# Layer 1 of a two-layer graph network: the end of a group in pairs of row tiles, 22 sums by transfer, head 3's last sum on GpSimd, and earlier loads of the row factors

## The chip, the core and the metric

The kernel runs on one core of one Trainium2 chip. A core has five engines with instruction streams of their own: TensorE (PE in the profile; PEld is its weight load), VectorE (DVE), ScalarE (ACT), GpSimd (POOL) and SyncE (SP), and 16 DMA engines that they share. A compute engine does its instructions in the order of its own stream. So does a queue of DMA issues: a DMA that has to wait for a semaphore holds back what stands behind it on the engine that issues it. The metric is device time in microseconds (us), from start to end of one execution.

## The reference

Layer 0 takes `x` (4096 x 512) and `adj` (4096 x 4096, zeros and ones) through a graph layer; the change doesn't touch it. Layer 1 is graph attention with 8 heads of 64 channels:

```python
h = relu(layernorm(x))
data1 = (h @ W.T + b).reshape(N, H, D)          # N = 4096, H = 8, D = 64
src = einsum('nhd,xhd->nh', data1, src_proj)
trg = einsum('nhd,xhd->nh', data1, trg_proj)
e = src.T[:, :, None] + trg.T[:, None, :]       # one number per head, row and column
e = where(e >= 0, e, 0.01 * e) + adj            # adj is added to the logits
scores = softmax(e, axis=-1)
out = einsum('hnm,hmd->hnd', scores, data1.transpose(1, 0, 2))
x = x + out                                     # heads side by side
```

## The kernel before

Layer 1 never forms the scores of all heads at once. It goes through 8 *groups*: 4 blocks of 1024 output rows (`WL`), each with 2 sets of 4 heads (`HG`). A group has 32 *steps* (`NT`), one for each tile of 128 columns `m`. In a step the kernel makes four unnormalised weight tiles `pr[i, m, k]`, 128 columns by 1024 rows, one for each head `k` of the set, and TensorE multiplies them with the values and adds up over the 32 steps in PSUM. The leaky relu under an exponential is a maximum of two products, so that a weight is `max(z, g) * exp(e)`, up to a factor of the column: `z` is a *row factor* (1024 numbers repeated on all partitions, one tile for each head, read again in all 32 steps), and `g` is one number per partition.

What each engine does in a step:

- SP (`load`, line 700): fetches the tile `e` of the adjacency for three steps ahead, into one of three buffers. A few steps also load the row factors of the next group (`zload`, line 695) or the row `u` (line 705). There are two sets of `z` tiles, used by groups in turn.
- ACT: `ex = exp(e)` (`exps`, line 718) into a single buffer in PSUM, so it can start only when VectorE has finished the step before; then, one step further ahead, `e3` (line 728), the same with head 3's factor of the column in it, and `rl` (line 746), a relu for head 0. In the first two groups it also scales two heads of the values (line 714).
- DVE (`weigh`): the four weight tiles in the order 3, 0, 1, 2 (lines 757 and 760). The instruction for head 3 reads `z` and `e3` from SBUF; the three others read `ex` from PSUM.
- In four steps, `BY_LOG`, head 0's tile is made without VectorE: ACT makes a relu of `u` (line 735), a DMA on GpSimd's queue adds the adjacency to it (line 736, issued five steps ahead), and ACT takes the exponential into `pr0` (line 743). VectorE then has three instructions in that step.
- POOL: adds head 3's tile to a running sum `acc3` (lines 767 and 769). For most steps it also issues a DMA that adds head 0's tile to one of two running sums in SBUF, by turns (`BY_DMA`, lines 774 and 776). `pr0` has three buffers, the other heads' tiles have two.
- PE (`gather`): 16 matmuls of 32 output columns for the product (line 792, "pv"), head pairs (3, 0) first, then (1, 2), and 4 with two output columns for the denominators of heads 1 and 2 (line 797, "dn"). Each is recorded as two. Four of them, in four column groups of the array, run side by side. For the steps that aren't in `BY_DMA` head 0's denominator is added here too, by two more matmuls for two of the four column groups (`by_pe`); which two alternates (`side`), and the order of the product's matmuls follows it. In the last step come head 3's last tile and the three running sums.

The program's order is written out by hand. A step `s` issues, in this order, `load` 3 steps ahead, `logs` 5, `exps` 1, `weigh` 1, `factors` 2, `scale` 2 and `gather` 0, and then the next piece of the end of the group before:

```python
stages = ((load, 3), (logs, 5), (exps, 1), (weigh, 1), (factors, 2), (scale, 2), (gather, 0))
```

The end of a group is spread over the first steps of the next one. At the end of `gather` ACT copies the product out of PSUM (line 821). `denominators` then copies the sums, turns them by eight small matmuls (line 831) and takes reciprocals on VectorE (line 835). After that `finish` works on 8 row tiles: `turn` (line 847) transposes one with two matmuls into the PSUM tile `pt`, which has one buffer, ACT multiplies its four heads by the reciprocals in the next step (line 871), GpSimd's queue adds the residual `x1` to two row tiles by one DMA (line 874), and SP stores them three steps later (line 877). In `finish` one row tile goes through in each of steps 2 to 9. The last group has its own end, `finish_last`, where PE turns all row tiles at once and ACT and VectorE share the scaling; tiles 4 to 7 lie in two PSUM banks.

Of the kernel before, what the change touches and what calls it, by code (L numbers as in the profile page):

```python
# [28 lines left out]
def kernel(  # L29
# [602 lines left out]

    HV = WL // BL
    JT = BL // P
    Q = P // 4
    BY_LOG = (17, 21, 25, 29)
    BY_DMA = [m for m in range(2, NT - 5) if m % 4 != 1]  # L640

    with tc.tile_pool(name="p", bufs=2) as prp, tc.tile_pool(name="rl", bufs=2) as rlp, tc.tile_pool(
        name="io1", bufs=3
# [48 lines left out]
        def zload(i, k):  # L692
            b, g = groups[i]
            zs_[i, k] = (zp1 if i % 2 else zp0).tile([P, WL], FP, name=f"z{k}")
            nc.sync.dma_start(zs_[i, k], row_bcast(z_d, WL, (g * HG + k) * N + b * WL))

        def load(i, m):
            b, g = groups[i]
            e = ep.tile([P, WL], FP, name="e")
            nc.sync.dma_start(e, adj_t[m * P:(m + 1) * P, b * WL:(b + 1) * WL])  # L700
            ra[i, m] = e
            if i + 1 < len(groups) and m == 28:
                us[i + 1] = usp.tile([P, WL], FP, name="u")
                b, g = groups[i + 1]
                nc.sync.dma_start(us[i + 1], row_bcast(u_d, WL, g * N + b * WL))
            if i + 1 < len(groups) and m in (20, 22, 24, 26):
                zload(i + 1, ORDER[(m - 20) // 2])

        def scale(i, m):

# [38 lines left out]
        def weigh(i, m, order=ORDER):  # L749
# [15 lines left out]
            if m == 1:  # L765
                acc[i, 3] = acp.tile([P, WL], FP, name="acc3", bufs=1)
                nc.gpsimd.tensor_tensor(acc[i, 3], pr[i, 0, 3], w, ALU.add)
            elif 1 < m < NT - 1:
                nc.gpsimd.tensor_tensor(acc[i, 3], acc[i, 3], w, ALU.add)  # L769
            if m in BY_DMA:  # L770
                n = BY_DMA.index(m)
# [6 lines left out]
        def gather(i, m):  # L778
# [26 lines left out]
                for q in range(HV):  # L805
                    den(side * HV + q, zo[:, 1 - side:3], pr[i, m, 0], q, start=False, stop=False)
            if last:
                for q in range(HV):
                    den(HV + q, zo[:, 1:3], pr[i, m, 3], q, start=False, stop=False)
                for q in range(HV):  # L810
                    den(q, zo[:, 1:3], acc[i, 0, 1], q, start=False, stop=False)
                for r, a in enumerate((acc[i, 0, 0], acc[i, 3])):
                    for q in range(HV):
                        den(r * HV + q, zo[:, 1:3], a, q, start=False, stop=True)
# [41 lines left out]
        def finish(i):  # L856


            dens = denominators(i)
            os_ = next(dens)  # L860
            yield
            next(dens)
            yield
            rd = next(dens)
            pts, os2 = {}, {}
            for t in range(WT + 4):
                if 0 < t <= WT:
                    if t % 2:
                        o = iop.tile([P, 2, HG, D], FP, name="o")
                    for r, k in enumerate(ORDER):  # L870
                        nc.scalar.activation(o[:, (t - 1) % 2, k, :], pts[t - 1][:, r, :], AF.Copy,
                                             scale=share(rd, t - 1, r))
                    if t % 2 == 0:
                        nc.gpsimd.dma_start(o, part(x1, i, t - 2, 2), accum_op=ALU.add)
                        os2[t] = o
                if t - 3 in os2:
                    nc.sync.dma_start(part(out, i, t - 5, 2), os2[t - 3])
                if t < WT:
                    pts[t] = p_t.tile([P, HG, D], FP, name="pt")
                    turn(os_, t, pts[t])  # L880
                yield

        def finish_last(i):

# [5 lines left out]
            os_ = next(dens)  # L890
            pts = [p_v.tile([P, HG, D], FP, name=f"pv{c}{q}") for q in range(HV) for c in range(2)]
            xs = p_x.tile([P, 4, HG, D], FP, name="ex")
            pts += [xs[:, n, :, :] for n in range(4)]
            for t in range(4):
                turn(os_, t, pts[t])
            next(dens)
# [115 lines left out]
```

## Time and profile before

The median of three runs is 2970.18 us (2969.84 to 2971.4). The profiled execution took 2974.0 us; its span, from the first instruction to the last, is 2972.2 us.

| | before |
|---|---|
| median of the runs | 2970.18 us |
| the profiled execution, its span | 2974.0 us, 2972.2 us |
| VectorE's first weight tile of layer 1 starts at | 1742.05 us |
| groups 0 to 7 start at (VectorE, head 3, step 0) | 1742.05, 1894.46, 2046.95, 2196.78, 2349.36, 2499.29, 2651.82, 2801.81 us |
| last step of the last group starts at | 2947.60 us |
| busy over the span: PE, DVE, ACT, POOL | 99%, 85%, 45%, 46% |
| DMA share of the time in groups 1 to 6 | 0.83 to 0.84 |

A start is that of VectorE's instruction for head 3, with which each step begins. The shares over the whole span mix two layers with different limits, so layer 1 is read by itself: busy times of the engines over whole groups, and the times of the steps within a group. PE's busy time counts a matmul from its modelled start to its modelled end, and neighbours overlap; how long a step takes PE is read from the start of one step's first matmul to that of the next. Records of a DMA issue stand on the engine that issues it; the landing is told separately.

### The profile page before, as it was taken

How to read it: one execution, taken by the hardware profiler on the slowest of the kernel's cores; microseconds unless marked ns; L12 is line 12 of the kernel's file. 1: busy time of each engine (PE TensorE's matmuls, PEld its weight loads, DVE VectorE, ACT ScalarE, POOL GpSimd, SP SyncE). 2: the span in 40 equal slices, each digit the busy share in tenths (PEclk: the TensorE clock that was granted, in tenths of full speed). 3: DMA queues.
4: the chain of work that ended last, by engine and by line, in shares of the span. 5: the costliest groups of instructions: out<-in, count | busy, mean ns of one | idle time of the engine just before them, and what ended most of it. 6: DMA issues, size and time to landing. Idle time of an engine off the chain costs nothing.

```text
span 2972.2 us, 43109 instructions
## 1 busy us (share of the span) xinstructions
PE 2930.7 (99%) x15371; PEld 1159.4 (39%) x15371; DVE 2522.1 (85%) x3596; ACT 1326.1 (45%) x1852; POOL 1376.0 (46%) x1042
## 2 busy tenths in 40 slices
PE   8999999999999999999999989999999999999998
PEld 4444444444444444444444423323222322232222
DVE  5434777778888888888897789999999999999998
ACT  2121111111122122122122368888777777777776
POOL 3401111113444444444443656575757575757574
PEclk9999999999999999999999999999999999999999
DMA  4205666667976675665553149696969696979795
GB/s 155 96 7 179 223 222 219 230 219 184 208 180 172 159 177 173 157 175 177 155 179 99 54 138 239 183 255 192 251 196 247 201 248 202 241 206 240 209 230 154
DMA packets 454056, 552.02 MB, mean 186 GB/s; under 512 B 261624, under 2 KB 287256, under 8 KB 453840
## 3 DMA queue, kind: packets, MB, share of 16 engines
q1 hardware_dynamic: 400816, 387.81, 42.2%
q0 software_dynamic: 51008, 157.51, 23.0%
q10 hardware_dynamic: 2016, 3.93, 0.4%
q8 instruction: 121, 1.98, 0.3%
q14 instruction: 95, 0.78, 0.1%
HBM read 409.47 MB, written 59.97 MB: 158 GB/s over the span
## 4 chain that ended last, share of the span: by engine, by line
PE 85%; DVE 6%; DMA 4%; ACT 2%; issue 2%; POOL 1%; SPq 0%; DVEq 0%; ACTq 0%; POOLq 0%
PE po L437 30%; PE pv L792 20%; PE pe L288 15%; PE dn L797 7%; DVE pr L760 5%; PE ps L159 4%; PE po L507 4%; PE pe L166 4%; DMA acc<-pr 2%; DMA e<-in_adj_t_dram 1%; DVE pr L757 1%; PE pt L847 1%; ACT e L728 1%; POOL acc L769 1%; ACT ex L718 0%
## 5 line engine op out<-in xcount | busy, mean ns | idle before, releaser
L792 PE MATMUL pv<-pr,sup 128*32 128x512 f32 x8192 | 1010.4, 595 | 10.3 <-POOL d_m L957 5.4
L437 PE MATMUL po<-sup,at 128*128 128x512 f32 x2048 | 886.7, 594 | 2.2 <-DVE at L407 2.2
L769 POOL TENSOR_TENSOR acc<-acc,pr 128x1024 f32<-128x1024 f32 x232 | 559.2, 2410 | 315.4 <-DVE pr L760 314.9
L760 DVE SCALAR_TENSOR_TENSOR pr<-z,g_m,ex 128x1024 f32<-128x1024 f32 x512 | 630.7, 1272 | 7.9 <-ACT ex L718 7.5
L437 PEld LDWEIGHTS po<-sup,at 128*128 128x128 f32 x2048 | 387.4, 190 | 480.7 <-issue 446.1
L417 POOL TENSOR_TENSOR racc<-racc,ex 128x512 f32<-128x512 f32 x240 | 358.3, 1493 | 390.7 <-ACT ex L401 389.0
L792 PEld LDWEIGHTS pv<-pr,sup 128*32 128x32 f32 x8192 | 288.5, 110 | 594.6 <-issue 528.2
L401 ACT ACTIVATE ex<-d 128x512 f32<-128x512 f32 x256 | 160.5, 630 | 664.7 <-DVE d L399 648.1
L288 PE MATMUL pe<-he_t,he_t 128*128 128x512 f32 x896 | 386.4, 592 | 0.0
L718 ACT ACTIVATE ex<-e 128x1024 f32<-128x1024 f32 x256 | 263.0, 1027 | 219.7 <-DVE pr L760 219.4
L760 DVE SCALAR_TENSOR_TENSOR pr<-z,g_m,e 128x1024 f32<-128x1024 f32 x256 | 328.3, 1282 | 9.3 <-PE pv L792 5.4
L797 PE MATMUL dn<-pr,d_m 128*2 128x512 f32 x1984 | 335.4, 592 | 0.0
L728 ACT ACTIVATE e<-e,ld_m 128x1024 f32<-128x1024 f32 x256 | 291.3, 1138 | 17.7 <-DMA e<-in_adj_t_dram 17.5
L757 DVE SCALAR_TENSOR_TENSOR pr<-rl,ngd_m,ex 128x1024 f32<-128x1024 f32 x224 | 284.8, 1271 | 1.9 <-ACT ex L718 1.5
L746 ACT ACTIVATE rl<-z,ngd_m,d_m 128x1024 f32<-128x1024 f32 x224 | 275.1, 1228 | 0.0
L407 DVE TENSOR_TENSOR at<-ex,a 128x512 f32<-128x512 f32 x256 | 195.3, 763 | 80.0 <-ACT ex L401 51.2
L288 PEld LDWEIGHTS pe<-he_t,he_t 128*128 128x128 f32 x896 | 169.2, 190 | 210.1 <-issue 190.5
L291 ACT COPY es<-pe 128x512 f32<-128x512 f32 (+2 forms) x144 | 79.3, 551 | 377.0 <-PE pe L288 377.0
L292 POOL DMA_DIRECT2D e_d<-es x144 | 78.5, 545 | 364.7 <-ACT es L291 359.2
L399 DVE TENSOR_TENSOR d<-pt,mk 128x512 f32<-128x512 f32 x256 | 176.9, 691 | 8.8
L293 DVE CUSTOM_DVE_ANT_0 mk<-pe,mk 128x512 f32<-128x512 f32 (+2 forms) x144 | 93.0, 646 | 99.3 <-ACT es L291 99.3
L392 DVE TENSOR_SCALAR mk<-a 128x512 f32<-128x512 f32 x256 | 136.5, 533 | 1.9 <-DMA a<-in_adj_t_dram 1.9
(173 smaller groups left out, 2595.0 us busy)
## 6 DMA issues: line engine op xcount, KB each, us to landing
e<-in_adj_t_dram SPq DMA_DIRECT2D x256, 512.0 KB, 5.5
acc<-pr POOLq DMA_DIRECT2D x152, 512.0 KB, 5.8
a<-in_adj_t_dram SPq DMA_DIRECT2D x256, 256.0 KB, 3.3
ar<-in_adj_dram SPq DMA_DIRECT2D x120, 256.0 KB, 3.1
e_d<-es POOLq DMA_DIRECT2D x120, 256.0 KB, 3.1
eb<-e_d SPq DMA_DIRECT2D x456, 64.0 KB, 2.7
ac<-in_adj_t_dram SPq DMA_DIRECT2D x112, 256.0 KB, 3.6
et<-e_d SPq DMA_DIRECT2D x112, 256.0 KB, 3.4
```

Of the source, the lines that this page charges most:

```text
L288: nc.tensor.matmul(pe[:, :w], he_t[i][:, k, (t % TB) * P:(t % TB + 1) * P], he_t[j][:, k, BL - w:], start=(k == 0), stop=(k == KC - 1))
L407: nc.vector.tensor_tensor(w, e, aj.pop((b, m)), ALU.mult)
L417: nc.gpsimd.tensor_tensor(racc, racc, e, ALU.add)
L437: nc.tensor.matmul(po[j], w[:, j * P:(j + 1) * P], sup[:, m, :], start=(m == 0), stop=last)
L718: nc.scalar.activation(x_, ra.pop((i, m)), AF.Exp)
L728: nc.scalar.activation(x_, ra[i, m], AF.Exp, bias=ld_m[:, h // HG, m:m + 1])
L746: nc.scalar.activation(r, zs_[i, 0], AF.Relu, bias=ngd_m[:, h // HG, m:m + 1], scale=d_m[:, h, m:m + 1])
L757: nc.vector.scalar_tensor_tensor(w, rl.pop((i, m)), ngd_m[:, h // HG, m:m + 1], x_, op0=ALU.subtract, op1=ALU.mult)
L760: nc.vector.scalar_tensor_tensor(w, zs_[i, k], g_m[:, h + k, m:m + 1], e3.pop((i, m)) if k == 3 else x_, op0=ALU.max, op1=ALU.mult)
L769: nc.gpsimd.tensor_tensor(acc[i, 3], acc[i, 3], w, ALU.add)
L792: nc.tensor.matmul(v[c][q][r * D + c0:r * D + c0 + Q, :], va[:, m, g * HG + k, c0:c0 + Q], pr[i, m, k][:, q * BL:(q + 1) * BL], start=(m = ...
L797: nc.tensor.matmul(dn[r * Q:r * Q + w.shape[1], :], w, src[:, q * BL:(q + 1) * BL], **fl)
```

## The change

Five things are changed, all in layer 1:

1. `BY_DMA` goes from 19 of the 32 steps to 22: all of 2 to 29 but 9, 13, 15, 18, 22 and 26. The steps whose denominator of head 0 is left to PE are now 0, 1, 9, 13, 15, 18, 22, 26, 30 and 31 (before: 0, 1, 5, 9, 13, 17, 21, 25 and 27 to 31).
2. `BY_LOG` moves from steps 17, 21, 25, 29 to 16, 20, 24, 28.
3. The row factors of the next group are loaded along with the tiles `e` of steps 1 to 4 (steps 21 to 24 in group 0), and not with 20, 22, 24 and 26.
4. GpSimd adds head 3's tile of step 31 to `acc3`; the two matmuls that PE had for it are gone.
5. `finish` takes row tiles by pairs, every third step: four transposes after steps 2, 5, 8 and 11, into a `pt` of twice the size; the scaling of one tile in each of the two steps that follow; the residual's DMA in steps 4, 7, 10 and 13; the stores in steps 6, 9, 12 and 15. In `finish_last` the row tiles 4 to 7 are placed so that 4 and 6 share one bank of PSUM and 5 and 7 the other.

```diff
-    BY_LOG = (17, 21, 25, 29)
-    BY_DMA = [m for m in range(2, NT - 5) if m % 4 != 1]
+    BY_LOG = (16, 20, 24, 28)
+    BY_DMA = [m for m in range(2, NT - 2) if m not in (9, 13, 15, 18, 22, 26)]
...
-            if i + 1 < len(groups) and m in (20, 22, 24, 26):
-                zload(i + 1, ORDER[(m - 20) // 2])
+            m0 = 1 if i else 21
+            if i + 1 < len(groups) and m0 <= m < m0 + 4:
+                zload(i + 1, ORDER[m - m0])
...
-            elif 1 < m < NT - 1:
+            elif m > 1:
                 nc.gpsimd.tensor_tensor(acc[i, 3], acc[i, 3], w, ALU.add)
...
             if last:
                 for q in range(HV):
-                    den(HV + q, zo[:, 1:3], pr[i, m, 3], q, start=False, stop=False)
-                for q in range(HV):
                     den(q, zo[:, 1:3], acc[i, 0, 1], q, start=False, stop=False)
...
-            pts, os2 = {}, {}
-            for t in range(WT + 4):
-                if 0 < t <= WT:
-                    if t % 2:
-                        o = iop.tile([P, 2, HG, D], FP, name="o")
-                    for r, k in enumerate(ORDER):
-                        nc.scalar.activation(o[:, (t - 1) % 2, k, :], pts[t - 1][:, r, :], AF.Copy,
-                                             scale=share(rd, t - 1, r))
-                    if t % 2 == 0:
-                        nc.gpsimd.dma_start(o, part(x1, i, t - 2, 2), accum_op=ALU.add)
-                        os2[t] = o
-                if t - 3 in os2:
-                    nc.sync.dma_start(part(out, i, t - 5, 2), os2[t - 3])
-                if t < WT:
-                    pts[t] = p_t.tile([P, HG, D], FP, name="pt")
-                    turn(os_, t, pts[t])
+            old = None
+            for t in range(0, WT, 2):
+                pt = p_t.tile([P, 2, HG, D], FP, name="pt")
+                for j in range(2):
+                    turn(os_, t + j, pt[:, j, :, :])
+                yield
+                o = iop.tile([P, 2, HG, D], FP, name="o")
+                for j in range(2):
+                    for r, k in enumerate(ORDER):
+                        nc.scalar.activation(o[:, j, k, :], pt[:, j, r, :], AF.Copy, scale=share(rd, t + j, r))
+                    if j == 0:
+                        if t:
+                            nc.sync.dma_start(part(out, i, t - 2, 2), old)
+                        yield
+                nc.gpsimd.dma_start(o, part(x1, i, t, 2), accum_op=ALU.add)
+                old = o
                 yield
+            yield
+            nc.sync.dma_start(part(out, i, WT - 2, 2), old)
+            yield
...
-            pts += [xs[:, n, :, :] for n in range(4)]
+            pts += [xs[:, n, :, :] for n in (0, 2, 1, 3)]
```

## The prediction

> **What bounds the kernel now.** The page first: over the whole span PE looks like the bound.
>
> ```profile
> span 2972.2 us, 43109 instructions
> ...
> PE 2930.7 (99%) x15371; PEld 1159.4 (39%) x15371; DVE 2522.1 (85%) x3596; ACT 1326.1 (45%) x1852; POOL 1376.0 (46%) x1042
> ```
>
> That average mixes the layers. The second view is the busy time in windows that are one group of layer 1 each (group 1, and the sum of 1 to 6; columns: us, PE, PEld, DVE, ACT, POOL, clock, DMA share, GB/s).
>
> ```profile
> 1894.46:2046.95 152.49, 151.93 (x1380) 47.85 (x1376) 149.10 (x127) 130.49 (x199) 95.23 (x57) 1.00 0.84 221
> ...
> sum 907.35, PE 906.44 PEld 273.19 DVE 893.68 ACT 714.48 POOL 570.97; mean PE 151.07 PEld 45.53 DVE 148.95 ACT 119.08 POOL 95.16
> ```
>
> Two engines are full: a group takes 907.35 / 6 = 151.2 us, PE is busy for 151.1, VectorE for 149.0. The timelines tell which leads where. On VectorE:
>
> ```profile
> 2252.09 1.27 DVE L757 SCALAR_TENSOR_TENSOR pr<-rl,ngd_m,ex 128x1024 f32<-128x1024 f32 x1
> 2253.30 2.47 DVE L760 SCALAR_TENSOR_TENSOR pr<-z,g_m,ex 128x1024 f32<-128x1024 f32 x2
> 2256.43 1.28 DVE L760 SCALAR_TENSOR_TENSOR pr<-z,g_m,e 128x1024 f32<-128x1024 f32 x1 [0.66 <-PE pv L792]
> ```
>
> Undisturbed, weight tiles start 1.193 us apart, a step takes 4.77 and a step by logs (three tiles) 3.58. The floor of a group is 28 x 4.77 + 4 x 3.58 = 147.9 us, and the last line shows one of the gaps above it, a wait for PE. Subtracting the floor from the start of each step on this timeline gives an excess of 4.5, 4.6, 1.9, 4.7, 2.0, 4.6, 2.1 and 2.6 us in groups 0 to 7, 26.9 together. It lies in four places (sums over groups): step 0 and 1 4.9 and 1.5, steps 7 to 12 7.6, steps 21 to 29 9.3, the reciprocal in step 3 1.3; the rest is 0.05 to 0.1 after each step by logs. The change removes no VectorE work, so it can win these gaps and the tail, no more.
>
> PE's timeline shows why step 11 has a gap (the starts of "pv" x32 are the starts of steps 9 and 10 of group 4; step 8 started at 2395.31):
>
> ```profile
> 2400.11 3.64 PE L792 MATMUL pv<-pr,sup 128*32 128x512 f32 x32
> 2403.57 1.04 PE L797 MATMUL dn<-pr,d_m 128*2 128x512 f32 x8
> 2404.43 1.03 PE L797 MATMUL dn<-pr,zo 128*3 128x512 f32 x4
> 2405.39 0.44 PE L847 MATMUL pt<-ident,os 128*128 128x128 f32 x2
> 2405.75 3.64 PE L792 MATMUL pv<-pr,sup 128*32 128x512 f32 x32
> ```
>
> A step with two transposes takes 4.80 us, with a denominator of head 0 as well 5.64; steps 11 and 12 without either take 4.29. So a pair of transposes costs 0.51 (the transposes start 0.11 apart at the tail, eight in 1.09; the rest is emptying the array) and a denominator 0.85. Where no transposes lie between two denominators on opposite column groups, they share one 0.85: step 13 takes 4.30 and step 17 5.14. PE falls behind VectorE from 4.9 us (step 1) to 8.1 (step 10); at about 7.5 head 3's buffers run out.
>
> Waits in layer 1, and DMA issues in a quiet stretch (2332 to 2358 us) and in the stretch with the row factors (2430 to 2480; last number: us to landing):
>
> ```profile
> ACT e L728 <- DMA e<-in_adj_t_dram: 17.5, 22, 1.9
> ...
> DVE pr L760 <- ACT ex L718: 7.5, 9, 1.9
> ...
> ACT pr L743 <- DMA acc<-pr: 7.1, 8, 2.0
> ```
>
> ```profile
> e<-in_adj_t_dram SPq DMA_DIRECT2D x6, 512.0 KB, 3.9
> ```
>
> ```profile
> e<-in_adj_t_dram SPq DMA_DIRECT2D x11, 512.0 KB, 8.3
> acc<-pr POOLq DMA_DIRECT2D x8, 512.0 KB, 8.8
> z<-z_d SPq DMA_DIRECT2D x4, 512.0 KB, 9.9
> ```
>
> The gaps of steps 21 to 29 come from here: with row factors under way everything lands twice as late, ACT waits for `e` or for `pr0` to be read out, and VectorE for ACT. Group 7, which loads none, has no gap in steps 13 to 29 beyond 0.06 after each step by logs.
>
> **The change, part by part.**
>
> *PE.* Before, the denominators cost ten times 0.85 a group: 0 with 1, 5, 9, four pairs (13/17, 21/25, 27/28, 29/30), and three rounds in step 31. After, seven: 0 with 1, 9 (step 11's transposes part it from 13), 13/15, 18/22, 26/30, two rounds in step 31 (31's own is on the other column groups). That is 3 x 0.85 = 2.6 us less. Transposes: 8 x 0.51 = 4.1 become 4 x (0.51 + 2 x 0.11) = 2.9. PE's group goes from 151.1 to 151.1 - 2.6 - 1.2 = 147.3, under VectorE's floor, so PE stops setting the pace: steps 7 to 12 lose their gap (7.6, all of it in groups 1 to 7). The cover is the lag: it rises by 0.9 to step 3 and falls 3.2 below the start by step 28, then rises; from the least lag seen, 2.8 in group 0, the peak is near 6, short of 7.5.
>
> *Head 3's last sum on GpSimd.* Step 1's head 3 tile waits now until PE has read head 3's tile of step 31 for the denominators (gap 0.4 to 0.8). Afterwards that buffer is free after the product. GpSimd is idle for 12.4 us at this place, its sum takes 2.4 and ends 3.7 after step 31 starts; PE needs it some 8 after. ACT's four copies out of PSUM (2.0 us) stay: ACT's step of 3.13 + 2.02 = 5.15 is longer than 4.77, and 0.27 of the gap stays. Saved: 0.2 to 0.5 in each of groups 1 to 7.
>
> *Loads of the row factors.* They leave the crowded steps and go behind the `e` loads at the seam of two groups, where an `e` lands in 3.9 us and has 9.4 (from its issue to head 3's exponential). On SP's queue the first waits for VectorE's head 3 tile of step 31, 0.1 later than the `e` behind it could start: nothing. The seven loads of `u` stay. Three more sums by DMA come, 0.6 of a step's DMA time each; four row factors of about 0.2 go from the crowd. I count the gaps of steps 21 to 29 in groups 1 to 6 as gone (7.2) but 0.7 in group 1, where ACT also scales values. In group 0 the loads come in four steps running, in the crowd: unchanged, 4.5.
>
> *The end by pairs.* VectorE's reciprocal stays, 0.18. ACT: an undisturbed step costs 3.13, four scalings 0.90, a relu for the logs 1.04. The relu for step 16 is issued in step 11, right behind the scalings of step 10: 5.07 + 0.11 against 4.77. Step 12 gets a new gap of about 0.26; group 1 has 0.55 of value scaling on top there and at the seam, 1.2 in all. Stores: SP now meets each one two steps after the residual's DMA, not three. That DMA took 4.1 or 8.0 us, the longer behind a sum; all four are behind a sum now. SP is held to 7.7 us into the next step, the `e` queued there could start at 6.0, so it goes 2.1 late and must land in 7.3. It landed in 5 to 8 in those steps: 0.3 a group.
>
> *The tail.* PE ends nearer VectorE: the lag of 5.33 us in the last step becomes some 3.6, and one round of 0.85 is gone: 2.5. The order of PSUM tiles 4 to 7 saves nothing: ACT's and VectorE's waits on one another stand in the changed program as before; 1.5 at best if they fell.
>
> **Weighing a rule.** Row: in step 17 of group 3 GpSimd's sum began late, behind a DMA issue, and ran on after VectorE's head 3 tile had started; that one took 1.94 instead of 1.28 and ended 1.10 after the sum.
>
> ```profile
> 2283.97 1.94 DVE L760 SCALAR_TENSOR_TENSOR pr<-z,g_m,e 128x1024 f32<-128x1024 f32 x1
> ```
>
> The Trainium skill, page "SBUF — State Buffer", section "Who interferes with whom", says why: a VectorE instruction with two inputs in SBUF and a GpSimd instruction that reads SBUF exclude each other for a whole instruction. By that rule the added sum speaks against the change, up to 2.4 us in each of 8 groups, 19 us, if it fell on a head 3 tile; by the row's times it ends 1.1 us before the next one starts, so it costs nothing, and the 0.06 after each step by logs stays.
>
> **Sum.** Groups 2 to 6: floor 147.88 + 0.18 + 0.27 + 0.26 + 0.25 (four steps after logs) + 0.3 = 149.1, five times; group 1: 151.0; group 0: 152.4; group 7 to the start of its last step: 149.1 - 4.77 = 144.3. Together 1193.2 against 2947.60 - 1742.05 = 1205.6: 12.4 less, with the tail 14.9. The profiled execution goes from 2974.0 to about 2959.1; the median stands 3.8 below it, so 2955.3. Bounds: every gap gone but group 0's start and the reciprocals, tail 3.5: 27 less, 2943. Gaps of steps 21 to 29 all kept: 6.5 worse, 2962.
>
> **Rivals.**
>
> 1. *The transfers stay late.* 22 sums instead of 19 put back what the row factors took out. For: steps 14 to 16 already show a DMA share near 0.95 with a sum and an `e` in each. Against: there the sums landed in 5 to 6 us, and they have 7.9 before ACT's `pr0`. 2962.
> 2. *Slower: SP stuck behind the stores.* If the residual's DMA lands at its worst seen, 9.9 us, the `e` behind goes 4 late and at 8 us to landing comes 2.6 after ACT wants it; ACT can absorb 1.5 of its idle time a step. 28 stores at 1.1 are 31 us against the 15 won: 2986. It decides against the change from 0.55 us a store on. For: stores already waited 20.0 us for the residual in 16 of 28 cases. Against: the longest such wait was 2.7, and the crowd thins.
> 3. *Nothing changes.* PE's relief is real but each freed gap is taken by ACT, whose step is 4.0 to 5.2 us in the first twelve steps: 2968 to 2972.
> 4. *All gaps go*: 2946.
>
> **How the numbers follow.** Main case 0.62, first rival 0.15, second 0.10, third 0.08, fourth 0.05. Within 0.2% (5.9 us) is what a measurement of this kernel can't tell from no change: 2964.2 to 2976.1. Faster 0.80 (main, fourth, most of the first), same 0.10, slower 0.10. The range leaves out the second rival, most of the third and the far end of the fourth: 2945 to 2966. The likeliest time is 2955.
>
> **What would show it.** Groups 2 to 6 of about 149 us with VectorE busy to 99% and PE showing waits for it; no wait of VectorE for PE in steps 8 and 12; `e` under 7 us to landing in steps 17 to 27; about 0.2 us before VectorE's second tile in steps 1 and 12; a tail of 22 us after the last step's start, not 24.6. Wrong if VectorE still waits for PE (my lag is off), if ACT waits for `e` behind the stores, or if a head 3 tile takes 1.9 us in each group.

## The result, and the profile after

The changed kernel takes 2978.70 us (median of 9 runs, 2975.83 to 2982.48) against 2970.66 (9 runs, 2969.73 to 2971.92): a ratio of 1.0028, 95% interval 1.0018 to 1.0038. It is slower by 8 us; 2955 was forecast, 15 faster. The profiled execution took 2979.28 us.

First the page of the changed kernel.

```profile
span 2977.5 us, 42931 instructions
...
PE 2918.4 (98%) x15243; PEld 1149.5 (39%) x15243; DVE 2521.6 (85%) x3596; ACT 1323.3 (44%) x1852; POOL 1411.3 (47%) x1074
```

PE lost 12 us of busy time and the span grew by 5. Where it grew shows in the windows of groups 2 and 3 and the sum of groups 1 to 6 (us, PE, PEld, DVE, ACT, POOL, clock, DMA share, GB/s).

```profile
2049.87:2202.43 152.56, 150.22 (x1356) 43.82 (x1356) 148.91 (x127) 116.37 (x137) 100.22 (x61) 1.00 0.91 233
2202.43:2353.64 151.21, 149.26 (x1356) 43.37 (x1356) 148.92 (x127) 116.28 (x137) 100.34 (x61) 1.00 0.91 233
...
sum 914.36, PE 899.55 PEld 264.08 DVE 893.69 ACT 711.98 POOL 601.25; mean PE 149.92 PEld 44.01 DVE 148.95 ACT 118.66 POOL 100.21
```

VectorE's work is what it was (893.69 against 893.68), but the six groups take 914.36 instead of 907.35. The DMA share rose from 0.83 or 0.84 to 0.90 or 0.91. So VectorE waits more, and no longer for PE. The waits of the changed kernel in layer 1 (us in total, times, longest):

```profile
PEld pv L792 <- DVE pr L760: 85.8, 147, 1.2
...
ACT e L728 <- DMA e<-in_adj_t_dram: 33.2, 26, 4.0
ACT pr L743 <- DMA acc<-pr: 24.6, 13, 3.0
DVE pr L760 <- ACT ex L718: 20.6, 20, 2.1
```

The kernel before had in the same list:

```profile
PEld pv L792 <- DVE pr L760: 27.3, 85, 1.1
...
DVE pr L760 <- PE pv L792: 5.4, 10, 0.7
```

VectorE's wait for PE (5.4 us before) is gone from the list, and PE's weight loads wait for VectorE for 85.8 us (27.3 before). In its place ACT waits for transfers: for the tile `e` 33.2 us against 17.5, for the sums of head 0 24.6 against 7.1, and VectorE waits for ACT (20.6 us against 7.5). The chain that ended last says the same. By line, its shares of the span, in the kernel before and in the changed one:

```profile
PE po L437 30%; PE pv L792 20%; PE pe L288 15%; PE dn L797 7%; DVE pr L760 5%; PE ps L159 4%; PE po L507 4%; PE pe L166 4%; DMA acc<-pr 2%; DMA e<-in_adj_t_dram 1%; DVE pr L757 1%; PE pt L847 1%; ACT e L728 1%; POOL acc L769 1%; ACT ex L718 0%
```

```profile
PE po L437 30%; PE pe L288 15%; DVE pr L760 10%; PE pv L792 6%; DMA acc<-pr 4%; PE ps L159 4%; PE po L507 4%; PE pe L166 4%; DMA e<-in_adj_t_dram 3%; ACT e L728 3%; PE dn L797 2%; DMA o<-x 2%; POOL acc L769 1%; ACT ex L718 1%; DVE pr L757 1%
```

The product of layer 1 (`pv`) had 20% and has 6; the sums by transfer went from 2 to 4%, `e` from 1 to 3, and the residual's transfer is new there.

By steps, the excess over VectorE's floor (the time of the steps beyond their undisturbed lengths, as in the prediction) is 37.0 us in the eight groups, where it was 26.9. Two places hold what is new. **Steps 20 and 28** have 13.9 (nothing before): these are logs steps now. **Steps 10 to 16** have 9.9, of which 1.9 in step 12 are ACT's as forecast; these are the steps of the stores. The gaps of steps 7 and 11 for PE are gone.

The first place, in group 2, on the timeline (start, us, engine and line, tiles; releaser in brackets):

```profile
2165.38 0.86 POOL L736 DMA_DIRECT2D lg<-in_adj_t_dram  x1 [0.27 <-ACT lg L735]
...
2169.03 0.86 POOL L776 DMA_DIRECT2D acc<-pr  x1
...
2172.68 0.85 POOL L776 DMA_DIRECT2D acc<-pr  x1
...
2183.63 1.15 ACT L743 ACTIVATE pr<-lg,t_m 128x1024 f32<-128x1024 f32 x1 [2.98 <-DMA acc<-pr]
...
2185.72 2.47 DVE L760 SCALAR_TENSOR_TENSOR pr<-z,g_m,ex 128x1024 f32<-128x1024 f32 x2 [1.24 <-ACT ex L718]
```

```profile
2172.68 10.77 DMA acc<-pr
```

Step 24, a logs step, is short (3.58 us). GpSimd's queue issues the logs' transfer for step 28, the sum of step 24 and the sum of step 25 within 7.3 us. The last of them lands after 10.77 us (second fence, from the chain). Head 0's tiles have three buffers, so step 28's goes over step 25's, which that sum reads, and ACT wanted it 2.98 us earlier; its `ex`, on which VectorE waits 1.24 us, stands behind.

The second place, also in group 2: SP's queue.

```profile
2102.32 0.39 SPq L875 DMA_DIRECT2D out_dram<-o  x1
...
2102.81 6.46 SPq L699 DMA_DIRECT2D e<-in_adj_t_dram  x3
...
2107.26 1.44 POOL L877 DMA_DIRECT2D o<-x  x1
...
2111.46 1.15 ACT L728 ACTIVATE e<-e,ld_m 128x1024 f32<-128x1024 f32 x1 [2.55 <-DMA e<-in_adj_t_dram]
...
2117.78 0.39 SPq L875 DMA_DIRECT2D out_dram<-o  x1
...
2118.28 6.26 SPq L699 DMA_DIRECT2D e<-in_adj_t_dram  x3
```

The store of 2117.78 follows a residual issued at 2107.26 that landed 10.51 us later, and two `e` loads come in a bunch behind it; behind the store before it, an `e` was 2.55 us late for ACT. Over all groups, what the stores waited for (the second line is a group's last store):

```profile
SPq L875 <- DMA o<-x: 155.7, 21, 8.4
SPq L881 <- DMA o<-x: 50.4, 7, 7.8
```

That is 206 us in all 28 cases; before it was 20.0 in 16. The `e` load behind a store was issued 3.2 us after its buffer had come free, on average over the 28; in the kernel before 0.03.

### The profile page after: what moved, and what is told of

It reads as the page before. It is cut to its first block, busy times and chain, and to the rows that moved or that the text cites. A ratio compares the mean times of both kernels' runs of the same rounds, so it can differ in the third digit from the quotient of the medians.

```text
span 2977.5 us, 42931 instructions
## 1 busy us (share of the span) xinstructions
PE 2918.4 (98%) x15243; PEld 1149.5 (39%) x15243; DVE 2521.6 (85%) x3596; ACT 1323.3 (44%) x1852; POOL 1411.3 (47%) x1074
## 4 chain that ended last, share of the span: by engine, by line
PE 65%; DVE 12%; DMA 10%; ACT 7%; issue 4%; POOL 2%; SPq 0%; DVEq 0%; ACTq 0%; POOLq 0%
PE po L437 30%; PE pe L288 15%; DVE pr L760 10%; PE pv L792 6%; DMA acc<-pr 4%; PE ps L159 4%; PE po L507 4%; PE pe L166 4%; DMA e<-in_adj_t_dram 3%; ACT e L728 3%; PE dn L797 2%; DMA o<-x 2%; POOL acc L769 1%; ACT ex L718 1%; DVE pr L757 1%
## 5 line engine op out<-in xcount | busy, mean ns | idle before, releaser
L792 PE MATMUL pv<-pr,sup 128*32 128x512 f32 x8192 | 1025.7, 595 | 21.7 <-DVE pr L760 10.3
L769 POOL TENSOR_TENSOR acc<-acc,pr 128x1024 f32<-128x1024 f32 x240 | 584.4, 2435 | 318.4 <-DVE pr L760 316.6
L760 DVE SCALAR_TENSOR_TENSOR pr<-z,g_m,ex 128x1024 f32<-128x1024 f32 x512 | 630.8, 1272 | 20.9 <-ACT ex L718 20.6
L797 PE MATMUL dn<-pr,d_m 128*2 128x512 f32 x1984 | 343.9, 592 | 0.0
L728 ACT ACTIVATE e<-e,ld_m 128x1024 f32<-128x1024 f32 x256 | 291.2, 1137 | 33.4 <-DMA e<-in_adj_t_dram 33.2
L776 POOL DMA_DIRECT2D acc<-pr x160 | 148.9, 931 | 0.1
```

The lines of the kernel that those rows point to most:

```text
L728: nc.scalar.activation(x_, ra[i, m], AF.Exp, bias=ld_m[:, h // HG, m:m + 1])
L760: nc.vector.scalar_tensor_tensor(w, zs_[i, k], g_m[:, h + k, m:m + 1], e3.pop((i, m)) if k == 3 else x_, op0=ALU.max, op1=ALU.mult)
L792: nc.tensor.matmul(v[c][q][r * D + c0:r * D + c0 + Q, :], va[:, m, g * HG + k, c0:c0 + Q], pr[i, m, k][:, q * BL:(q + 1) * BL], start=(m = ...
L797: nc.tensor.matmul(dn[r * Q:r * Q + w.shape[1], :], w, src[:, q * BL:(q + 1) * BL], **fl)
```

## The experiments

All times are medians. "Beside" is the kernel before on the same chip; the chip differs between the groups of runs, so differences are taken to that. An "excess" is that of the profiled execution, by steps as in the prediction. Theory A is the first place (sums of the logs steps late), theory B the second (stores on SP's queue), theory C the whole transfer load.

| kernel | us | beside | ratio (95%) | excess |
|---|---|---|---|---|
| changed | 2978.70 | 2970.66 | 1.0018 to 1.0038 | 37.0 |
| changed, sums as before | 2967.34 | 2971.86 | 0.9971 to 0.9989 | 20.0 |
| changed, end as before | 2969.21 | 2971.86 | 0.9985 to 1.0002 | 23.8 |
| changed, logs steps by PE | 2963.38 | 2971.86 | 0.9956 to 0.9980 | 21.1 |
| changed, stores later | 2972.07 | 2971.86 | 0.9992 to 1.0010 | 29.2 |
| both of these | 2960.63 | 2971.13 | 0.9952 to 0.9979 | 16.9 |
| both, group 0's loads spread | 2959.58 | 2971.13 | 0.9949 to 0.9974 | 16.2 |
| changed, loads as before | 2988.67 | 2971.13 | 1.0047 to 1.0073 | 49.3 |
| before, loads alone | 2972.36 | 2971.13 | 0.9993 to 1.0011 | 25.9 |
| changed, steps after logs by PE | 2971.86 | 2971.94 | 0.9993 to 1.0010 | 27.2 |
| before, head 3's sum alone | 2970.70 | 2971.94 | 0.9989 to 1.0007 | 23.8 |
| before, 22 sums alone | 2980.03 | 2971.94 | 1.0019 to 1.0042 | 36.6 |
| before, pairs alone | 2970.18 | 2971.94 | 0.9989 to 1.0007 | 21.2 |
| steps after logs by PE, stores later | 2959.61 | 2971.67 | 0.9946 to 0.9973 | 17.8 |
| before, 22 sums, logs steps by PE | 2963.51 | 2971.67 | 0.9963 to 0.9986 | 18.3 |
| both, loads spread, end as before | 2959.14 | 2971.67 | 0.9945 to 0.9970 | 16.0 |

### Which part loses

The 19 sums and the logs steps of before, in the changed kernel:

```diff
-    BY_LOG = (16, 20, 24, 28)
-    BY_DMA = [m for m in range(2, NT - 2) if m not in (9, 13, 15, 18, 22, 26)]
+    BY_LOG = (17, 21, 25, 29)
+    BY_DMA = [m for m in range(2, NT - 5) if m % 4 != 1]
```

> The changed kernel with parts 1 and 2 undone: BY_DMA and BY_LOG as before, 19 sums by transfer. Theory A (the sums of the logs steps go by transfer now: the logs DMA, the sum of the logs step and that of the next step stand within 8 us on GpSimd's queue, land after 9 to 10 us, and ACT's head 0 tile of the next logs step waits): the gaps of VectorE in steps 20 and 28 (14.0 us over the groups) are gone, PE gets three denominators back and has room for them; about 2966. Theory B (SP held by the stores, the tiles e late): those gaps stay in another place, steps 10, 13 and 16 keep their 8.0 us; time within 4 us of 2978. Theory C (the load of the DMA engines as a whole, 0.91 of a group's time): three sums less bring the share to 0.84 and all gaps go together, steps 13 and 16 too: about 2958.

Measured 2967.34, 4.5 below the kernel beside it, nearest to A. B as the whole cause is ruled out here, though it is visible: ACT's wait for `e` stays at 27.6 us and the stores wait 168.

The group's end of before (`finish`), in the changed kernel:

```diff
-            for t in range(0, WT, 2):
-                pt = p_t.tile([P, 2, HG, D], FP, name="pt")
...
+            for t in range(WT + 4):
+                if 0 < t <= WT:
+                    if t % 2:
```

> The changed kernel with the end of a group as before (part 5 undone, finish_last as changed). Theory A: the gaps in steps 20 and 28 stay at 14 us, those in steps 10 to 16 (10 us) go, PE has 1.6 us more a group and still fits; about 2969. Theory B (the stores are the cause of all, since tiles e that come late push the transfers behind them): steps 20 and 28 shrink to under 4 us as well; about 2958. If pairs are what keeps PE out of VectorE's way, the old gap of 0.5 to 0.8 in steps 7 and 11 comes back: 2973.

Measured 2969.21, 2.7 below, as A expected. ACT's wait for `e` falls to 3.0 us, the stores' to 53.6. The wait for the sums stays at 15.7, but its gaps moved from steps 20 and 28 to step 24 (11.3 of the 23.8), which A did not expect; why they moved is not shown. No gap for PE came back in steps 7 to 12.

### The two places taken away

PE sums the logs steps in place of 15, 18, 22 and 26. There are still 22 sums by transfer, the same bytes:

```diff
-    BY_DMA = [m for m in range(2, NT - 2) if m not in (9, 13, 15, 18, 22, 26)]
+    BY_DMA = [m for m in range(2, NT - 2) if m not in (9, 13, 16, 20, 24, 28)]
```

> The changed kernel with 22 sums as there, but the steps left to PE are 0, 1, 9, 13, 16, 20, 24, 28, 30 and 31: the logs steps' own sums go to PE, and 15, 18, 22 and 26 go by transfer. The bytes moved are the same. Theory A: the crowd of three transfers at each logs step is broken up, head 0's buffer is read out in time, steps 20 and 28 lose 14.0 to under 3 us; about 2967. Theory C (the whole load): the same bytes, the same waits, within 3 us of 2978. Theory B: steps 10, 13 and 16 keep their 8 us.

Measured 2963.38, below what A expected. It is 8.5 below the kernel beside it, where the changed kernel was 8.0 above: 16.5 us between them, give or take 5 by the two intervals. Its waits:

```profile
ACT e L728 <- DMA e<-in_adj_t_dram: 37.4, 31, 2.8
...
ACT pr L743 <- DMA acc<-pr: 3.2, 4, 1.7
```

ACT's wait for the sums fell from 24.6 to 3.2 us at the same DMA share, 0.91. So it is the place of the sums among the transfers and not their load, and C is ruled out. The wait for `e` is untouched, which is B's.

Each store goes one step later, in the changed kernel:

```diff
                 for j in range(2):
...
                     if j == 0:
-                        if t:
-                            nc.sync.dma_start(part(out, i, t - 2, 2), old)
                         yield
                 nc.gpsimd.dma_start(o, part(x1, i, t, 2), accum_op=ALU.add)
+                if t:
+                    nc.sync.dma_start(part(out, i, t - 2, 2), old)
                 old = o
                 yield
             yield
+            yield
```

> The changed kernel with each store issued one step later (steps 7, 10, 13, 16: three steps after the residual's DMA as before the change, not two). Theory B: SP waits for the residual 206 us in 28 stores now; with a step more under 60; the gaps in steps 10, 13 and 16 (8.0 us) go to under 2; about 2972; if late tiles e also push the sums, steps 20 and 28 shrink too and it is 2965 or less. Theory A: steps 20 and 28 keep their 14 us. Theory C: nothing moves by more than 2 us.

Measured 2972.07, level with the kernel beside it: 7.8 us off the change. The stores wait 57.2 us instead of 206, ACT for `e` 6.6. The waits for the sums stay (19.7), again moved to step 24 (10.5).

Both edits together, in the changed kernel:

```diff
-    BY_DMA = [m for m in range(2, NT - 2) if m not in (9, 13, 15, 18, 22, 26)]
+    BY_DMA = [m for m in range(2, NT - 2) if m not in (9, 13, 16, 20, 24, 28)]
...
                     if j == 0:
-                        if t:
-                            nc.sync.dma_start(part(out, i, t - 2, 2), old)
                         yield
...
+                if t:
+                    nc.sync.dma_start(part(out, i, t - 2, 2), old)
                 old = o
                 yield
+            yield
             yield
```

> The changed kernel with two edits: the four logs steps (16, 20, 24, 28) are summed by PE in place of 15, 18, 22, 26 (22 sums by transfer stay), and each store of a pair of row tiles is issued one step later. Theory A (the sums of the logs steps, crowded by the logs' own transfer, land after ACT's head 0 tile wants their buffer) was worth 15.3 us when its edit stood alone (2978.7 to 2963.4), theory B (SP's queue held by the stores, `e` late) 6.6 alone (2978.7 to 2972.1). If they are two causes they add: 2978.7 - 15.3 - 6.6 = 2956.8, with an excess over VectorE's floor of about 13 us, no gap in steps 10 to 16 beyond ACT's 0.25 in step 12, and ACT's wait for the sums (L743 for `acc`) under 4 us. If they are one (the transfers are late, and each edit only moves where it shows), the second edit brings nothing on top: 2962 to 2965, and the gaps come back in step 24.

Measured 2960.63, 10.5 below: between the two expectations. The second edit brings 2.0 us on top of the first by the times, which their intervals don't tell from nothing, and 4.2 us of excess. So the two seem not to add in full: 18.5 us together, 16.5 and 7.8 alone; in excess 20.1 together, 15.9 and 7.8 alone. What stays is 16.9 us of excess, 5.1 of it in step 15, where VectorE writes head 0's tile over that of step 12: that sum, issued 3 us behind a logs' transfer, lands in 10 to 14 us (median 12.1). It looks like the first cause in small; no run takes this one away.

### The loads of the row factors

The kernel with both edits, and group 0's four loads spread over steps 20 to 26:

```diff
-            m0 = 1 if i else 21
-            if i + 1 < len(groups) and m0 <= m < m0 + 4:
-                zload(i + 1, ORDER[m - m0])
+            m0, dm = (1, 1) if i else (20, 2)
+            if i + 1 < len(groups) and m in range(m0, m0 + 4 * dm, dm):
+                zload(i + 1, ORDER[(m - m0) // dm])
```

> The kernel of the run before (logs steps by PE, stores one step later) with the row factors of group 0 loaded in steps 20, 22, 24, 26 in place of 21 to 24; the other groups stay. My prediction said that four loads in four crowded steps leave group 0 unchanged against the kernel before (4.5 us of excess); the changed kernel showed 6.8 in group 0, 4.3 of it in steps 23 and 24, behind a wait of 3.97 for `e` in ACT. If the spacing of these four loads is the cause, steps 23 and 24 of group 0 lose about 3 us and the time is 3 below the run before (about 2954). If it is the number of loads in the crowd and not their spacing, the gap spreads over steps 21 to 28 and the time is the same within 1.

Measured 2959.58, 11.6 below: 1 us better than without, which the intervals don't tell from nothing, and group 0's excess 4.0 instead of 5.2. The spacing is worth about 1 at most, not 3. The windows' sum for groups 1 to 6 of this kernel, and its waits:

```profile
sum 898.34, PE 889.73 PEld 262.55 DVE 891.40 ACT 712.15 POOL 600.72; mean PE 148.29 PEld 43.76 DVE 148.57 ACT 118.69 POOL 100.12
```

```profile
ACT e L728 <- DMA e<-in_adj_t_dram: 5.3, 8, 1.4
...
ACT pr L743 <- DMA acc<-pr: 1.6, 3, 0.7
```

A group takes 149.7 us, VectorE is busy for 148.6 of it.

The loads as in the kernel before, in the changed kernel:

```diff
-            m0 = 1 if i else 21
-            if i + 1 < len(groups) and m0 <= m < m0 + 4:
-                zload(i + 1, ORDER[m - m0])
+            if i + 1 < len(groups) and m in (20, 22, 24, 26):
+                zload(i + 1, ORDER[(m - 20) // 2])
```

> The changed kernel with the loads of the row factors where they were before (steps 20, 22, 24, 26 of every group). My prediction counted their move as 7.2 us won in groups 1 to 6. If the move is worth that beside the other parts, 2978.7 + 7 = 2986, minus about 3 for group 0's spacing: 2983. Theory A says that the gaps of the logs steps come from three transfers of GpSimd's queue within 7 us, and the loads on SP's queue come on top: ACT's wait for `acc` rises above 24.6 us and the time lies at 2980 to 2986. If the loads at steps 1 to 4 are what makes the residual's transfer and the stores late (theory B with another cause), steps 10 to 16 lose their 8 us, and the time is 2971 to 2976.

Measured 2988.67, above every expectation and 17.5 above the kernel beside it: the move of the loads is worth 9.5 us beside the other parts. Steps 20 and 24 alone have 26.6 us of excess (in an execution 4.8 above the median). Steps 13 to 16 keep their 8: the loads at the seam are not what delays the stores.

The change's loads alone, in the kernel before:

```diff
-            if i + 1 < len(groups) and m in (20, 22, 24, 26):
-                zload(i + 1, ORDER[(m - 20) // 2])
+            m0 = 1 if i else 21
+            if i + 1 < len(groups) and m0 <= m < m0 + 4:
+                zload(i + 1, ORDER[m - m0])
```

> The kernel before with one part of the change alone: row factors loaded in steps 1 to 4 (group 0: 21 to 24). My prediction's step on the loads says that the gaps of steps 21 to 29 in groups 1 to 6 (7.2 us) go: about 2963.5, and ACT's waits for `e` (17.5 us) and for `acc` (7.1) fall to under 10 together. If the loads only displace the trouble to the steps with the residuals and stores, or if the gaps of steps 21 to 29 have another cause (a sum beside the logs), the time is 2968 to 2973, and gaps of over 3 us stay in steps 21 to 29 or appear in steps 10 to 16.

Measured 2972.36, no change. Yet the step did what it said: the gaps of steps 21 to 29 went from 10.4 to 4.3 us. But those of steps 0 to 12 rose from 13.8 to 18.9 (the reciprocal of step 3 not counted). The windows' sum of groups 1 to 6 and VectorE's waits in this kernel (its lines are numbered one higher from 718 on):

```profile
sum 905.34, PE 905.05 PEld 264.49 DVE 893.73 ACT 713.38 POOL 570.44; mean PE 150.84 PEld 44.08 DVE 148.96 ACT 118.90 POOL 95.07
```

```profile
DVE pr L761 <- PE pv L793: 7.0, 13, 0.7
DVE pr L761 <- ACT os L822: 6.4, 7, 1.2
```

PE is busy for 905.05 of 905.34 us. In the kernel before PE sets the pace of a group, and what VectorE wins in steps 21 to 29 it waits for PE in the next group's first steps (3.4 us for ACT's copies behind PE before, 6.4 now).

### What makes a sum late

PE sums the step after a logs step, so that only two of the three transfers are left:

```diff
-    BY_DMA = [m for m in range(2, NT - 2) if m not in (9, 13, 15, 18, 22, 26)]
+    BY_DMA = [m for m in range(2, NT - 2) if m not in (9, 13, 17, 21, 25, 29)]
```

> The changed kernel with PE summing the steps that follow a logs step (17, 21, 25, 29) in place of 15, 18, 22, 26; the logs steps 16, 20, 24, 28 stay with the transfers, 22 in all. Theory A in its first form says that three transfers of GpSimd's queue within 8 us (the logs', the logs step's sum, the next step's sum) are the cause: with the third gone the gaps of steps 20 and 28 go as in the run with the logs steps by PE, 2963 to 2967, ACT's wait for `acc` under 5 us. If it is the logs step's own sum, issued right behind the logs' transfer and needed for the same buffer, that lands late without any help from the third, the wait for `acc` stays at 15 to 25 us and the time at 2973 to 2979.

Measured 2971.86, outside both expectations. ACT's wait for the sums is gone altogether, as A's first form says, but ACT now waits more for `e`, and steps 18 and 19 have 8.4 us of gaps:

```profile
ACT e L728 <- DMA e<-in_adj_t_dram: 46.0, 30, 4.1
```

The wait did not go because the sums became early. The logs steps' own sums of steps 20 and 24 land after 8.9 and 9.5 us here (medians of the groups), 8.7 and 9.5 in the changed kernel. In group 2, the sum of step 24 in the changed kernel and in this one:

```profile
acc<-pr POOLq DMA_DIRECT2D x1, 512.0 KB, 9.4
```

```profile
acc<-pr POOLq DMA_DIRECT2D x1, 512.0 KB, 9.0
```

What changed is who reads the buffer that ACT wants. The logs steps' tiles of 20, 24 and 28 go over those of 17, 21 and 25, and PE sums these now, so no transfer holds that buffer. With the logs steps by PE the sums of 17, 21 and 25 still hold it, but land after 6.7, 5.5 and 8.3 us instead of 9.6, 8.2 and 9.8.

The same with the stores one step later, so against the changed kernel:

```diff
-    BY_DMA = [m for m in range(2, NT - 2) if m not in (9, 13, 15, 18, 22, 26)]
+    BY_DMA = [m for m in range(2, NT - 2) if m not in (9, 13, 17, 21, 25, 29)]
...
                     if j == 0:
-                        if t:
-                            nc.sync.dma_start(part(out, i, t - 2, 2), old)
                         yield
...
+                if t:
+                    nc.sync.dma_start(part(out, i, t - 2, 2), old)
                 old = o
                 yield
+            yield
             yield
```

> The changed kernel with PE summing the steps behind the logs steps (17, 21, 25, 29) and each store one step later. Without the later stores ACT's wait for `acc` fell from 24.6 us to nothing, but the time only from 2978.7 to 2971.9, with new gaps in steps 18 and 19 (8.4 us) where ACT waits for `e`. If those come from SP's queue (theory B), the later stores take them away, and 2971.9 - 6.6 to 8.4 = 2963.5 to 2965.3, or less, down to the 2960.6 of the kernel with the logs steps by PE and later stores. If they come from the logs step's own sum in the crowd of transfers, they stay and it is 2969 to 2972.

Measured 2959.61, 12.1 below and lower than expected: the gaps were the stores' (ACT's wait for `e` falls to 8.4 us, the gaps of steps 18 and 19 go). So either of the two sums may leave. The logs step's own sum is late behind the logs' transfer with or without the third, but ACT's long waits come where the third, which holds its buffer, stands behind both. And the stores' price depends on what else is under way: 2.0, 7.8 and 12.0 us in the three pairs of kernels.

### The other parts alone

Head 3's last sum on GpSimd, in the kernel before:

```diff
-            elif 1 < m < NT - 1:
+            elif m > 1:
...
-                for q in range(HV):
-                    den(HV + q, zo[:, 1:3], pr[i, m, 3], q, start=False, stop=False)
```

> The kernel before with one part alone: head 3's last sum on GpSimd, one round of denominators less in step 31. My prediction's step: 0.2 to 0.5 in each of groups 1 to 7, and one round of 0.85 in the tail: 2970.7 - 2.3 to 4.4 = 2966.3 to 2968.4. If PE sets the pace of the kernel before from group to group, its group is 0.85 shorter and all of it shows: 7 x 0.85 = 6 and 0.85 in the tail, 2964. If the added sum meets a head 3 tile on VectorE (1.94 us in place of 1.28), 2971 or more, with such tiles in every group.

Measured 2970.70, 1.2 below (2.3 to 4.4 expected of the part), which the interval doesn't tell from nothing. In the profile the gap of step 0 goes from 4.9 to 0.7 and that of step 1 rises from 1.5 to 4.0. One head 3 tile of 256 took 1.94 us, as before.

The logs in steps 16, 20, 24 and 28 and the 22 sums, in the kernel before:

```diff
-    BY_LOG = (17, 21, 25, 29)
-    BY_DMA = [m for m in range(2, NT - 5) if m % 4 != 1]
+    BY_LOG = (16, 20, 24, 28)
+    BY_DMA = [m for m in range(2, NT - 2) if m not in (9, 13, 15, 18, 22, 26)]
```

> The kernel before with one part alone: logs in steps 16, 20, 24, 28 and 22 sums by transfer. PE has two denominators less (1.7 us a group), and the gaps of VectorE for PE in steps 0 to 12 (up to 12 us) shrink. If the sums' placement is harmless by itself, 2960 to 2965. Theory A says 14 us of waits for `acc` in the logs steps come in, and the row factors load in the same stretch, which in the run with the loads as before made it 35 us of ACT's waits: 2974 to 2985.

Measured 2980.03, 8.1 above: this part by itself loses as much as the whole change. PE's gaps are gone here too, and two waits pay for it:

```profile
ACT pr L743 <- DMA acc<-pr: 24.2, 13, 2.8
DVE pr L760 <- ACT ex L718: 21.4, 18, 2.4
```

The same with PE summing the logs steps:

```diff
-    BY_LOG = (17, 21, 25, 29)
-    BY_DMA = [m for m in range(2, NT - 5) if m % 4 != 1]
+    BY_LOG = (16, 20, 24, 28)
+    BY_DMA = [m for m in range(2, NT - 2) if m not in (9, 13, 16, 20, 24, 28)]
```

> The kernel before with the sums part alone, but PE sums the logs steps (9, 13, 16, 20, 24, 28; 22 by transfer). The part alone as the change has it took 2980.0. If its loss is the place of the four sums, the 15 us of the earlier run come off: about 2965, with ACT's wait for `acc` (24.2 us) under 5. If the row factors, which still load in steps 20 to 26, keep the transfers late whatever the place of the sums, it is 2970 to 2976.

Measured 2963.51, 8.2 below: the place of four sums is worth 16.3 us, as in the changed kernel (16.5), although the row factors still load beside them. The wait for the sums stays at 7.4, over the 5 expected.

The end by pairs alone (all of `finish` as the change has it), in the kernel before:

```diff
-            for t in range(WT + 4):
-                if 0 < t <= WT:
-                    if t % 2:
...
+            for t in range(0, WT, 2):
+                pt = p_t.tile([P, 2, HG, D], FP, name="pt")
```

> The kernel before with one part alone: a group's end by pairs of row tiles. My prediction's step: PE 1.2 us less a group, so most of the gaps of steps 7 to 12 go (6 of 7.6), against new gaps of ACT in step 12 (0.26 x 8 = 2.1) and 0.3 a group behind the stores (2.1): 2966 to 2969. Theory B says that the stores hold SP's queue: 1.1 us a group in steps 10 to 16, ACT's waits for `e` there above 15 us, 2971 to 2975.

Measured 2970.18, 1.8 below, between the two expectations and not told from nothing. All gaps for PE in steps 7 to 12 are gone (7.4 us), but steps 18 to 21 went from 3.3 to 12.1: ACT's wait for `e` is 33.1 us and the stores wait 163.

Last, the kernel of 2959.58 us (logs steps by PE, later stores, spread loads) with all of `finish` as in the kernel before:

```diff
-            for t in range(0, WT, 2):
-                pt = p_t.tile([P, 2, HG, D], FP, name="pt")
...
+            for t in range(WT + 4):
+                if 0 < t <= WT:
+                    if t % 2:
```

> The kernel of 2959.6 us (logs steps by PE, later stores, group 0's loads spread) with the group's end as in the kernel before, by single row tiles, stores three steps behind. My prediction's step gave PE 1.2 us a group from the pairs. With seven denominators PE's group is then 147.3 + 1.2 = 148.5, still at VectorE's pace of 149, so the pairs are worth nothing here: 2957 to 2962. If the pairs' relief of PE is needed, gaps for PE come back in steps 7 to 12 and it is 2964 or more.

Measured 2959.14, 12.5 below, with no gap for PE. The pairs bring nothing once three denominators are gone. This and the two other kernels near 2959.5 are faster than both the kernel before and the changed one (ratio to the kernel before 0.9957, 0.9945 to 0.9970).

## Why the prediction was wrong, step by step

**What bounds the kernel.** Right that the gaps lay in four places and that VectorE's floor is the limit. But the gaps were added up as if each could be won alone. With the loads moved alone, 6.1 us won in steps 21 to 29 brought 5.1 of new waits in steps 0 to 12.

**PE.** Right in what it decides. In the changed kernel a step takes PE 4.29 us, 5.00 with a pair of row tiles (0.71 more; 0.73 worked out), 5.14 with a denominator. PE's lag behind VectorE peaks at 6.48 us in step 3 of groups 2 to 7 (near 6 forecast), and the gaps of steps 7 and 11 are gone. That the peak fits is in part luck: from the start of a group to step 3 the lag rises by 2.0 us, not 0.9, and its least value in these groups is 1.9, not 2.8.

**Head 3's last sum.** Right in kind and size: with this part alone the gaps of steps 0 and 1 go from 6.4 to 4.7 us over the groups, 0.25 in each of the seven that follow another (0.2 to 0.5 forecast). On the weighed rule: one head 3 tile of 256 took 1.94 us in the changed kernel; a GpSimd sum was running when it started, and it ended 1.10 us after that sum. What the Trainium skill's page "SBUF — State Buffer", section "Who interferes with whom", says of VectorE and GpSimd excluding each other agrees with that tile. The added sums met no such tile, as the row's times had it.

**Loads of the row factors.** This step failed. Its own price was not too high: beside the other parts the move is worth 9.5 us (7.2 forecast). What failed is the sentence "I count the gaps of steps 21 to 29 in groups 1 to 6 as gone", with three more sums priced by their number, 0.6 of a step's DMA time each. The change also moves the logs steps' own sums from PE to the transfers. Before, each logs step left a free place on GpSimd's queue behind the logs' transfer. Now the logs' transfer, the logs step's sum and the next step's stand within 6.9 to 7.3 us (group 2), and the sums land in 7.9 to 10.8 us (groups 2 and 3), where ACT has 7.9 for the last of them. That costs 16.5 us with the same bytes. The first rival was of this kind, but it was refused with the sums of steps 14 to 16, which landed in 5 to 6, and bounded at "gaps all kept", 6.5 us: a bound that let the gaps stay, not grow.

**Group 0.** Forecast unchanged at 4.5 us of excess; it is 6.8. Spreading its loads brings some 1.

**The end by pairs.** ACT's new gap in step 12 was right (1.9 us in the seven groups that follow another: 0.18 in five of them, 0.36 and 0.66 in the two others; 0.26 forecast, and more in group 1). The stores were mis-sized: 0.3 a group forecast, 2.1 in the seven; 7.8 measured by the later stores. The residual's transfer was taken at 8.0 us and took 9.3 (median), so the stores held SP for 7.4 us each, and the `e` loads behind them went out 3.2 us late on average, where 2.1 was forecast. A sign that the prediction named for being wrong, ACT waiting for `e` behind the stores, came. The second rival had the mechanism, but its price does not decide by itself: without A's cause the change with the stores as they are gains 8.5 us.

**The tail.** 24.59 us became 21.27, 3.3 less (2.5 forecast). By the parts alone: the sums part 2.5, head 3's sum 0.4, the pairs 0.4.

**From the profile to the median.** The forecast took 3.8 us off because the profiled execution of the kernel before stood so far above its median. That is no constant: over the sixteen later kernels the difference runs from 2.4 below to 4.8 above, 0.3 on average.

With both causes removed the forecast's path comes out: from the first weight tile to the last step's start 1193.2 us were forecast, and the kernel with both edits and spread loads takes 1194.9, at 2959.58 us. So the rest of the sum held in its total. In part that is luck: 4.9 us lie in step 15, which the forecast did not have, while the stores' 2.1 are gone in this kernel and groups 0 and 1 came out 0.5 and 1.2 lower. The two terms named, 16.5 and 7.8 (18.5 together), are, with the 3.8, nearly all that separates 2955 from 2978.7.

Not shown is why a transfer of GpSimd's queue takes nearly twice as long when a logs' transfer, or that and a sum, stands close before it. The runs show when it does and what it costs, not what inside the DMA engines or the queue does it.

## What to carry to other kernels

Price a transfer by what stands beside it on its own queue at that place and by when its buffer is wanted, not by its share of the load. Where work goes from an engine to a queue, look first at which empty places of the queue it fills. A gap is won only if the next engine in line is not as late: put parts of a change on the old kernel one by one and their sum (here a loss of 6, near the change's own 8) does not tell what they bring with the four sums and the stores in other places (a gain of 12).

## What the runs showed of the hardware that was not expected

Transfers of 512 KB within SBUF that add to a sum took 4.6 to 5.9 us behind a step summed by PE (in 19, 23 and 27), and 7.9 to 10.8 in steps 16, 20 and 24 and the steps behind them, where a logs' transfer stands before them, in groups 2 and 3 of the changed kernel. In steps 28 and 29, where none does, the two sums took 5.2 to 5.5. The residual's transfer is half as large and took 9.3. In groups 1 to 6 (transfers, KB each, median us to landing) of the changed kernel:

```profile
acc<-pr POOLq DMA_DIRECT2D x132, 512.0 KB, 7.1
lg<-in_adj_t_dram POOLq DMA_DIRECT2D x24, 512.0 KB, 7.9
...
o<-x POOLq DMA_DIRECT2D x24, 256.0 KB, 9.3
```

and of the changed kernel with the logs steps by PE:

```profile
acc<-pr POOLq DMA_DIRECT2D x132, 512.0 KB, 6.0
lg<-in_adj_t_dram POOLq DMA_DIRECT2D x24, 512.0 KB, 8.7
...
o<-x POOLq DMA_DIRECT2D x24, 256.0 KB, 9.2
```

The same 132 sums land 1.1 us earlier in the median, at a DMA share of 0.91 in both. A share of 0.9 was no limit in itself: the fastest kernels here have 0.91 and 0.92.
